# One step table, fp8 transposes and a searched end list in a fused conv-scan, linear-attention and FFN kernel

## The chip, the cores and the metric

The kernel runs on one core of a Trainium2 chip, in one launch. The metric is the device time of one execution in microseconds. The time before is 1214.04 us, the median of three runs (1212.67 to 1214.79). The engines are called PE (TensorE, with PEld for its weight loads), DVE (VectorE), ACT (ScalarE), POOL (GpSimd) and SP (SyncE, which issues most DMAs).

## The reference, cut to what matters

The input is x of 4 images, 64 x 64 positions, 96 channels, in fp32. L below is the 4096 positions of an image.

```python
# layer 0: a selective scan over the positions of an image
xn   = layernorm(group_norm(x), eps=1e-3) * gamma + beta        # (4, 4096, 96)
proj = xn @ W_in + b_in                                         # 3*96 + 3*96*16 columns
value, gate, delta = proj[:96], sigmoid(proj[96:192]), proj[192:288]
A, B, C = the rest, each (L, 96, 16)
h[t] = delta[t] * A[t] * h[t-1] + delta[t] * B[t] * value[t]    # 16 states per channel
y[t] = gate[t] * sum_over_states(C[t] * h[t])
x = x + y @ W_out + b_out
# layer 1: attention without softmax, so it is a product of small matrices
t = x as tokens
t = t + attention(layernorm(t))        # 6 heads, q @ k.T @ v, then @ Wff + bff
# feed-forward with fp8 (e5m2) operands and fp16 results
q = layernorm(t) rounded to e5m2
h = relu(fp16(fp16(q @ W1q.T) + b1q))
t = t + fp16(fp16(e5m2(h) @ W2q.T) + b2q)
```

## The kernel before

An image is cut into 8 chunks of 512 positions, so there are 32 chunks. The 96 x 16 scan states of a chunk are 12 tiles of 128 states by 512 positions (3 groups of channels times 4 groups of states). Tile number k = 12 g + r stands for tile r of chunk g, and each tile is a step of the main loop; K = 384 is the number of steps.

What one step s issues is written out by hand in the loop at the end of the kernel. On PE it is the B projection of tile s+3, the A projection of s+1 and the C projection of s, each three matmuls of 512 columns (a high and a low part; `project`, L244). On DVE it is the scan of tile s (L767), a_mul of tile s+1 (L760, it reads and writes A's PSUM bank) and c_mul of tile s (L791). On POOL it is b_mul of tile s+2 (L751). On ACT it is b_copy of tile s+3 (L748) and the copy of a scan's last state (L777). In the steps whose r is in `ON_POOL` the product with C is not made on DVE: ACT copies C's projection out (L797, c_copy) and POOL multiplies (L800, c_mul_pool). There are two PSUM banks for A, one for B, one each for even and odd C, and three (M) shared by all the other pieces. There are five buffers for b_mul's tiles (bu) and three for scans (h).

All the other work of a chunk is made of pieces which `at(step, fn)` hangs onto a step; `call(s)` issues them behind the step's own work, in the order in which they were hung. There are four kinds:

- `front`, for layer 0's input: load_x, centre and scale (group norm, POOL), stats (DVE), rstd (POOL), apply (ACT), transpose (PE), affine and upper (ACT), low (DVE and DMAs), the projections of delta, value and gate (PE, with d_out, du_out, gate_out), and the write and read through DRAM that spreads delta and delta times value over the partitions (rep). Steps count from the constant `FRONT` = -22 ahead of the chunk.
- `group_norm`: for the next image, sums over a chunk (load_gx, four transposes, two ACT passes at L509) from `SUMS` = -28.
- `gather` and `tail`: DMAs on POOL's queue that add up the four tiles of states, then state_sum and project_out (PE), gated and residual (DVE), the second layer norm (stats, rstd, apply into xa), its transpose, copy and spill to DRAM, and the gram matrix, from which `attn_matrix` makes one 97 x 96 matrix per image.
- `ffn`, an image later, since it needs that matrix: fetch, attention (L982), residual, stats, rstd, apply (L371 on ACT, L378 `apply_vector` on DVE), four fp32 transposes (L996), quant_in to fp8 (L1000), three times hidden and relu, project_out, round_out, bias_out (L1049) and total (L1055) on POOL, store. Steps count from `FFN0` = 28 behind the step at which the next image's same chunk begins.

What falls on steps from K on is not hung onto a step: it goes to the list scheduler `Plan`, object `end`. It knows each job's engine, a cost in us written in the code, what it waits for and which buffers it takes. It goes through the jobs once: it starts the one that can start first, and within `LOOK` of that time it takes the lowest rank, then the longest chain behind. The whole feed-forward of image 3 is made there. Another `Plan` makes the first six steps of the kernel.

An x tile has 15 buffers (`XBUFS`); `total` is its last reader.

Of the kernel before, what the change touches and what calls it, by code (L numbers as in the profile page):

```python
# [37 lines left out]
FRONT = -22  # L38
SUMS = -28
FFN0 = 28  # L40
ON_POOL = (1, 3, 6, 10)
# [4 lines left out]
def conv_attn_hybrid_kernel(  # L46
# [35 lines left out]
        "xn2": 1, "xq": 1, "h16": 1, "hr": 1, "hq": 1, "y16": 1, "yb": 1, "o": 1,  # L82
# [106 lines left out]
    xa_t, xal_t = [], []  # L189
    for r in range(2):  # L190
        t = const.tile([P, J, CA], F32, tag=f"xa{r}", name=f"xa{r}")
        nc.gpsimd.memset(t[:, :, C:CA], 1.0)
        xa_t.append(t)
        t = const.tile([CA, J, P], F32, tag=f"xal{r}", name=f"xal{r}")
        nc.gpsimd.memset(t[C:CA], 1.0)
        xal_t.append(t)

# [12 lines left out]
    w2_sb = sb("xn2", [C, HID], F32, "w2_sb")  # L210
# [125 lines left out]
    class LayerNorm:  # L336
# [32 lines left out]
        def apply(self, dst, src):  # L369
            for j in range(J):  # L370
                nc.scalar.activation(  # L371
                    dst[:, j, 0:C], src[:, j, :], AF.Identity,
                    bias=self.nmr[:, j : j + 1], scale=self.r[:, j : j + 1],
                )

        def apply_vector(self, dst, src):
            for j in range(J):
                nc.vector.tensor_scalar(  # L378
                    dst[:, j, 0:C], src[:, j, :], self.mv[:, j, 0:1], self.r[:, j : j + 1],
                    ALU.subtract, ALU.mult,  # L380
                )
# [5 lines left out]
    class Plan:  # L387
        HOP = 0.15
        LOOK = 0.3

# [19 lines left out]
        def run(self, fill=None):  # L410
# [13 lines left out]
            taken, back = self.taken, {}  # L424
            todo = list(self.jobs)
            while todo:
                best = None
                for n, j in enumerate(todo):
                    if any(a["end"] is None for a in j["after"]):
                        continue  # L430
                    t = self.time.get(j["engine"], 0.0)
                    for a in j["after"]:
                        hop = 0.0 if a["engine"] == j["engine"] else self.HOP
                        t = max(t, a["end"] + a["late"] + hop)
                    full = False
                    for b in j["take"]:
                        r = b.split(":")[0]
                        if len(taken[r]) >= self.rings[r]:
                            k = taken[r][-self.rings[r]]
                            full = full or k not in back  # L440
                            t = max(t, back.get(k, 0.0) + self.HOP)
                    if full:
                        continue
                    key = (t, j["rank"], -tail(j), n)
                    if best is None or t < best[0][0] - self.LOOK or (
                        t < best[0][0] + self.LOOK and key[1:] < best[0][1:]
                    ):
                        best = key, j
                (t, _, _, n), j = best
                todo.pop(n)  # L450
# [5 lines left out]
                j["end"] = self.time[e] = t + j["cost"]  # L456
                for b in j["take"]:
                    taken[b.split(":")[0]].append(b)
                for b in j["free"]:
                    back[b] = j["end"] + j["late"]  # L460
# [103 lines left out]
    def group_norm(b, s0):  # L564
# [11 lines left out]
        when = [s0 + SUMS + NT * n for n in range(NCH)]  # L576
# [119 lines left out]
    def front(b, i, s0, f=None):  # L696
        s = s0 + FRONT
        if f is None:
            f = Front(b, i)
            if (b, i) not in xt:  # L700
                at(s - 3, load_x, b, i)
            at(s, f.centre, nc.gpsimd)
            at(s + 1, f.scale, nc.gpsimd)
            at(s + 2, f.stats)
            at(s + 3, f.ln.rstd)
            at(s + 5, f.apply)
            at(s + 7, f.transpose)
            at(s + 8, f.affine)
            at(s + 9, f.upper)
            at(s + 9, f.low)  # L710
            at(s + 12, f.proj, 2)
            at(s + 13, f.d_out)
            at(s + 13, f.proj, 0)
            at(s + 14, f.du_out)
            at(s + 14, f.write)
            at(s + 15, f.read)
        at(s + 20, f.proj, 1)
        at(s + 21, f.gate_out)
# [89 lines left out]
    def state_sum(g, last=None, first=None):  # L808
# [17 lines left out]
        {"A": 2, "B": 1, "C": 1, "M": 3, "xal": 2, "xat": 1, "bu": 5, "h": 3, "rep": 2,  # L826
# [3 lines left out]
    end.last = {}  # L830

    def tail(b, i, s0):


        nm, g = f"{b}_{i}", b * NCH + i
        v, ln = {}, LayerNorm(1e-5, f"a_{nm}")
# [46 lines left out]
        def gram_add():  # L883
            nc.gpsimd.tensor_tensor(grams[b], grams[b], v["add"], ALU.add)

        plan = [
            (5, state_sum, g), (6, gated), (7, project_out), (8, residual), (8, ln.stats, t),
            (9, ln.rstd), (12, ln.apply, xa, t), (14, transpose), (15, keep), (16, spill),
            (21, gram), (22, gram_out),
        ]  # L890
        if i:
            plan.append((23, gram_add))
        for n, fn, *args in plan:
            if s0 + n < K:
                at(s0 + n, fn, *args)
        if s0 + plan[-1][0] < K:
            return
# [3 lines left out]
        job, a = end.job, None  # L901
        if s0 == K:
            for sh, late in ((0, 0.0), (2, 0.0), (3, 2.4)):
                w = job(f"wait{sh}", late, lambda: None)
                a = job("PE", 0.5, state_sum, g, sh, sh > 0, after=[a, w],
                        take=["B:y"] if sh == 0 else [])
            a = job("DVE", 0.7, gated, after=[a], free=["B:y"])
            a = job("PE", 0.5, project_out, after=[a], take=["B:o"])
            a = job("DVE", 0.56, residual, after=[a], free=["B:o"])
            a = job("DVE", 1.1, ln.stats, t, after=[a], take=[f"mv:a{i}"])  # L910
            a = job("POOL", 1.3, ln.rstd, False, after=[a])
        else:
            job("wait", 0.0, lambda: None, take=[f"mv:a{i}"])
        if s0 == K:
            applied = job("DVE", 1.3, ln.apply_vector, xa, t, after=[a], free=[f"mv:a{i}"])
        else:
            applied = job("ACT", 1.55, ln.apply, xa, t, free=[f"mv:a{i}"])
        a = job("PE", 0.4, gram, after=[applied, end.last.get("gram")], take=[f"B:g{i}"])
        end.last["gram"] = job("DVE", 0.25, gram_sum, after=[a], free=[f"B:g{i}"])
        a = job("PE", 0.45, transpose, after=[applied], take=[f"C:a{i}"])  # L920
        a = job("ACT", 0.57, keep, after=[a], free=[f"C:a{i}"], take=[f"xat:{i}"])
        end.last[b, i] = job("SP", 0.5, spill, after=[a], late=2.5, free=[f"xat:{i}"])
# [4 lines left out]
    def attn_matrix(b, s0):  # L927
# [31 lines left out]
        for n, (args, out) in enumerate(chain):  # L959
            if s0 < K:  # L960
                at(s0 + 24 + n, mm, *args)
                at(s0 + 24 + n, out)
            else:
                a = end.job("PE", 0.3, mm, *args, after=[a], take=[f"B:r{n}"])
                a = end.last["r"] = end.job("DVE", 0.25, out, after=[a], free=[f"B:r{n}"])

    def ffn(b, i, s0):
# [6 lines left out]

        def fetch():
            v["xa"] = xal_t[i % 2]
# [12 lines left out]
        def apply():  # L989
            v["xn"] = tile_of("xn2", "bu", [P, J, C], F32, "xn2")  # L990
            (ln.apply_vector if b == B - 1 else ln.apply)(v["xn"], t)

        def transpose():
            ps = v["ps"] = bank("C" if phase["end"] else "M", [C, TC], f"xq_ps_{nm}")
            for j in range(J):
                nc.tensor.transpose(ps[:, j * P : (j + 1) * P], v["xn"][:, j, :], ident)  # L996

        def quant_in():
            v["xq"] = tile_of("xq", "h", [C, TC], F8, "xq")
            nc.scalar.activation(v["xq"], v["ps"], AF.Copy, saturate=False)  # L1000
# [7 lines left out]
        def relu(m):  # L1008
            if m == 0:
# [37 lines left out]
        def bias_out():  # L1047
            v["yb"] = tile_of("yb", "xl", [P, J, C], F16, "yb")
            nc.gpsimd.tensor_tensor(  # L1049
# [3 lines left out]
        def total():  # L1053
            v["o"] = tile_of("o", "z", [P, J, C], F32, "o")
            nc.gpsimd.tensor_tensor(v["o"], t, v["yb"], ALU.add)  # L1055

        def store():
            nc.sync.dma_start(out_v[b, i], v["o"])

        plan = [  # L1060
            (min(-4, K - 4 - s0) if b < B - 1 else 0, fetch),
            (0, attention), (1, residual), (1, ln.stats, t), (2, ln.rstd),
            (5, apply), (7, transpose), (8, quant_in),
            (9, hidden, 0), (10, relu, 0), (11, hidden, 1), (12, relu, 1),
            (13, hidden, 2), (14, relu, 2), (15, project_out), (16, round_out),
            (17, bias_out), (18, total), (19, store),
        ]
        done = [fn for n, fn, *args in plan if s0 + n < K]
        for n, fn, *args in plan:
            if s0 + n < K:  # L1070
                at(s0 + n, fn, *args)
# [4 lines left out]
        end.rank = 1 + b * NCH + i  # L1076
        assert relu not in done
        if fetch in done and attention not in done:
            end.hold(f"xal:{nm}")

        def job(engine, cost, fn, *args, **kw):
            if fn not in done:
                return end.job(engine, cost, fn, *args, **kw)
            return None
# [5 lines left out]
        a = job("DVE", 1.1, ln.stats, t, after=[a], take=[f"mv:{nm}"])  # L1090
        vector = b == B - 1
        a = job("POOL", 1.3 if vector else 1.8, ln.rstd, not vector, after=[a])
        a = job("DVE" if vector else "ACT", 1.3 if vector else 1.55, apply, after=[a], take=[f"bu:x{nm}"], free=[f"mv:{nm}"])
        a = job("PE", 0.45, transpose, after=[a], take=[f"C:{nm}"], free=[f"bu:x{nm}"])
# [267 lines left out]
```

## Time and profile before

| | |
|---|---|
| median of three runs | 1214.04 us |
| profiled execution | 1214.51 us, of which the span is 1212.8 us |
| busy share of the span | PE 95%, DVE 93%, POOL 85%, PEld 72%, ACT 67% |
| mean granted TensorE clock | 0.989 |
| first scan starts, last scan ends | 30.77 us, 1135.71 us |
| chain that ended last | DVE 3%, PE 1%, POOL 1%, issue 1%; it begins at 1129.95 us |

The page gives busy time by engine, and groups of equal instructions with their count, busy time and mean length; times in groups are us, means ns. In the timeline each line has its start and its length in us, engine, line, operation and tiles. Instructions of one engine overlap: a matmul of 512 columns is shown 0.39 us long while the next starts 0.23 us behind it, so what an instruction takes of an engine is the distance to the next start. The waits name the waiting engine, line and tile, whom it waited for, the time in total, how often, and the longest.

### The profile page before, as it was taken

To read this page: it belongs to the slowest core of one execution; us is meant where nothing else is said; L and a number is where in the kernel's file an instruction comes from. 1 tells how busy PE (TensorE), PEld (TensorE's weight loads), DVE (VectorE), ACT (ScalarE), POOL (GpSimd) and SP (SyncE) were. 2 spreads that over 40 slices of the span, in tenths; PEclk is the share of its full clock that TensorE was granted. 3 is DMA by queue.
4 is the path that set the end of the run, shared out by engine and by line. 5 is a ranking of instruction groups with operands and counts; after the bars stand their busy time and mean duration, and the time that the engine had idled before them with its cause. 6 is when DMAs were issued, how large, how long until landed. Compare 5 with 4: busy or idle time off the path is not lost. (4 is left out here: it accounts for less than half of the span.)

```text
span 1212.8 us, 19189 instructions
## 1 busy us (share of the span) xinstructions
PE 1155.5 (95%) x5888; PEld 872.8 (72%) x5888; DVE 1125.7 (93%) x2103; ACT 809.9 (67%) x1812; POOL 1031.6 (85%) x1171
## 2 busy tenths in 40 slices
PE   6899999999999999999999999999999999999884
PEld 5677777777777777777777777677777777777652
DVE  6799999999999999999999999999999999999794
ACT  4655656655565787777777777777777777776574
POOL 3988878888888888999999888999999899988654
PEclk8999999999999999999999999999999999999998
DMA  7656767677776676677667766766776667666221
GB/s 185 141 133 145 165 151 164 147 161 164 168 160 151 153 166 151 154 168 176 159 151 164 172 154 146 174 154 149 154 174 154 154 158 174 153 145 142 66 66 40
DMA packets 104289, 182.14 MB, mean 150 GB/s; under 512 B 42637, under 2 KB 50769, under 8 KB 104186
## 3 DMA queue, kind: packets, MB, share of 16 engines
q1 hardware_dynamic: 90060, 106.96, 36.5%
q0 software_dynamic: 13536, 73.93, 30.2%
q8 instruction: 47, 0.77, 0.3%
q14 instruction: 56, 0.46, 0.1%
q10 hardware_dynamic: 590, 0.02, 0.0%
HBM read 69.12 MB, written 24.77 MB: 77 GB/s over the span
## 5 line engine op out<-in xcount | busy, mean ns | idle before, releaser
L751 POOL TENSOR_TENSOR bu<-bu,rep 128x512 f32<-128x512 f32 x384 | 557.7, 1496 | 14.7 <-ACT bu L748 9.2
L748 ACT ACTIVATE bu<-Bps,b_bac 128x512 f32<-128x512 f32 x384 | 263.7, 687 | 286.0 <-PE Bps L244 269.0
L767 DVE TENSOR_TENSOR_SCAN h<-Aps,state,bu 128x512 f32<-128x512 f32 x336 | 426.4, 1269 | 13.2 <-POOL bu L751 3.5
L760 DVE SCALAR_TENSOR_TENSOR Aps<-Aps,b_bac,rep 128x512 f32<-128x512 f32 x384 | 282.5, 736 | 25.1 <-PE Aps L244 24.6
L244 PE MATMUL Bps<-xs,w 128*128 128x512 f32 x768 | 268.1, 430 | 3.7 <-ACT bu L748 3.4
L244 PE MATMUL Aps<-xs,w 128*128 128x512 f32 x768 | 249.6, 406 | 14.2 <-DVE h L767 13.3
L800 POOL TENSOR_TENSOR ch<-ch,h 128x512 f32<-128x512 f32 x128 | 193.5, 1512 | 2.6 <-ACT ch L797 2.4
L244 PEld LDWEIGHTS Aps<-xs,w 128*128 128x128 f32 x768 | 138.6, 189 | 70.5 <-DVE h L767 42.3
L244 PEld LDWEIGHTS Bps<-xs,w 128*128 128x128 f32 x768 | 129.4, 191 | 46.5 <-issue 24.3
L244 PE MATMUL Aps<-xl,w 128*128 128x512 f32 x384 | 152.6, 397 | 0.3 <-DMA w<-w 0.3
L244 PE MATMUL Bps<-xl,w 128*128 128x512 f32 x384 | 151.8, 395 | 0.0
L244 PE MATMUL Dps<-xs,w 128*128 128x512 f32 x384 | 121.1, 397 | 0.0
L244 PE MATMUL Cps<-xs,w 128*128 128x512 f32 x384 | 120.8, 395 | 0.0
L806 POOL DMA_DIRECT2D ch<-ch x94 | 89.0, 947 | 15.1 <-DMA ch<-ch 11.5
L791 DVE SCALAR_TENSOR_TENSOR ch<-Dps,b_bac,h 128x512 f32<-128x512 f32 x128 | 94.7, 740 | 0.5 <-PE Dps L244 0.4
L791 DVE SCALAR_TENSOR_TENSOR ch<-Cps,b_bac,h 128x512 f32<-128x512 f32 x128 | 95.0, 742 | 0.0
L244 PEld LDWEIGHTS Aps<-xl,w 128*128 128x128 f32 x384 | 72.4, 188 | 18.4 <-DMA w<-w 1.0
L244 PEld LDWEIGHTS Bps<-xl,w 128*128 128x128 f32 x384 | 72.5, 189 | 17.5
L244 PEld LDWEIGHTS Dps<-xs,w 128*128 128x128 f32 x384 | 72.4, 189 | 17.5
L244 PEld LDWEIGHTS Cps<-xs,w 128*128 128x128 f32 x384 | 72.3, 188 | 17.5
L244 PE MATMUL Dps<-xl,w 128*128 128x512 f32 x192 | 76.0, 396 | 0.0
L244 PE MATMUL Cps<-xl,w 128*128 128x512 f32 x192 | 75.7, 394 | 0.0
(196 smaller groups left out, 2056.0 us busy)
## 6 DMA issues: line engine op xcount, KB each, us to landing
ch<-ch POOLq DMA_DIRECT2D x94, 768.0 KB, 6.5
rep<-ddd SPq DMA_DIRECT2D x124, 384.0 KB, 6.4
ddd<-dd SPq DMA_DIRECT2D x31, 384.0 KB, 3.0
xl<-lo SPq DMA_DIRECT2D x62, 128.0 KB, 2.4
x<-in_x_dram SPq DMA_DIRECT2D x32, 192.0 KB, 2.9
xatd<-xat SPq DMA_DIRECT2D x32, 192.0 KB, 3.1
xal<-xatd SPq DMA_DIRECT2D x32, 192.0 KB, 5.8
out_dram<-o SPq DMA_DIRECT2D x32, 192.0 KB, 2.1
```

The costliest lines, as they stand in the source:

```text
L244: nc.tensor.matmul(ps, lhsT=wt[:, n], rhs=mv, start=(n == 0), stop=(n == 2))
L748: nc.scalar.activation(self.bu, self.b_ps, AF.Identity, bias=self.bias(0))
L751: nc.gpsimd.tensor_tensor(self.bu, self.bu, rep[self.b, self.i][:, 1, self.cg], ALU.mult)
L760: nc.vector.scalar_tensor_tensor(self.a_ps, self.a_ps, self.bias(1), rep[self.b, self.i][:, 0, self.cg], ALU.add, ALU.mult,)
L767: nc.vector.tensor_tensor_scan(self.h, self.a_ps, self.bu, 0.0 if self.i == 0 else state[self.sh, self.cg], ALU.mult, ALU.add,)
L791: nc.vector.scalar_tensor_tensor(self.slot(), self.c_ps, self.bias(2), self.h, ALU.add, ALU.mult)
L800: nc.gpsimd.tensor_tensor(self.ch, self.ch, self.h, ALU.mult)
L806: nc.gpsimd.dma_start(chs[g, 0], chs.pop((g, sh)), accum_op=ALU.add)
```

## The change

1. `FRONT`, `SUMS`, `FFN0` and the steps written in the functions are replaced by one table `AT`, with a step for each piece; nearly every piece gets another step. `ON_POOL` is (0, 2, 7, 8) instead of (1, 3, 6, 10).
2. In the feed-forward, apply writes fp8 directly (two lasting tiles xn8 of 128 x 4 x 128, zeroed once), and the four transposes are fp8 matmuls with an fp8 identity; quant_in reads the first 96 partitions. hidden 1 runs at step 31, a while ahead of hidden 0 and 2.
3. `Plan.run` makes its list by a function `schedule(bias, look)`; for the end it tries 800 lists with random ranks added and keeps the one whose last job ends first by the costs. The costs of several jobs differ, all ffn chunks of four share a rank, and the rules for what falls into the end are by groups (`place`).
4. In the end, the feed-forward's norm of image 3 is applied by DVE for even chunks and by ACT for odd ones, where DVE had all; bias_out and total of the last two chunks are on DVE.
5. The start's `LOOK` is 0.6 instead of 0.8.

```diff
-FRONT = -22
-SUMS = -28
-FFN0 = 28
-ON_POOL = (1, 3, 6, 10)
+AT = {
+    "load_x": -39, "centre": -25, "scale": -24, "stats": -22, "rstd": -22, "apply": -21,
+    "transpose": -14, "affine": -13, "upper": -13, "low": -12, "proj_d": -9, "d_out": -9,
+    "proj_u": -9, "du_out": -9, "write": -9, "read": -6, "proj_gate": -3, "gate_out": -1,
+    "gather1": 7, "gather2": 11, "gather3": 14,
+    "state_sum": 18, "gated": 18, "project_out": 19, "residual": 19, "stats_a": 20,
+    "rstd_a": 21, "apply_a": 22, "transpose_a": 33, "keep": 34, "spill": 39, "gram": 24,
+    "gram_out": 24, "gram_add": 26,
+    "fetch": 21, "attention": 26, "residual_f": 26, "stats_f": 26, "rstd_f": 27, "apply_f": 29,
+    "transpose_f": 30, "quant_in": 31, "hidden0": 37, "relu0": 37, "hidden1": 31, "relu1": 33,
+    "hidden2": 38, "relu2": 38, "project_f": 40, "round_out": 40, "bias_out": 40, "total": 46,
+    "store": 51,
+    "sums": -31,
+}
+ON_POOL = (0, 2, 7, 8)
...
+        vector = b == B - 1 and i % 2 == 0
...
         def apply():
-            v["xn"] = tile_of("xn2", "bu", [P, J, C], F32, "xn2")
-            (ln.apply_vector if b == B - 1 else ln.apply)(v["xn"], t)
+            v["xn"] = next_of(xn8_t, "xn8")
+            (ln.apply_vector if vector else ln.apply)(v["xn"], t, saturate=False)

         def transpose():
-            ps = v["ps"] = bank("C" if phase["end"] else "M", [C, TC], f"xq_ps_{nm}")
+            ps = v["ps"] = bank("C" if phase["end"] else "M", [P, TC], f"xq_ps_{nm}")
             for j in range(J):
-                nc.tensor.transpose(ps[:, j * P : (j + 1) * P], v["xn"][:, j, :], ident)
+                nc.tensor.matmul(
+                    ps[:, j * P : (j + 1) * P], lhsT=v["xn"][:, j, :], rhs=ident8,
+                    start=True, stop=True,
+                )
...
+            last_two = phase["end"] and b == B - 1 and i > NCH - 3
...
+            rng = random.Random(1)
+            best = zero = [0.0] * len(self.jobs)
+            lates = schedule(zero, self.LOOK)
+            for n in range(self.tries):
+                wide = n < self.tries // 4
+                share, size = (1.0, rng.choice((0.5, 2.0, 5.0))) if wide else (0.02, 2.0)
+                bias = [
+                    b + rng.gauss(0.0, size) if rng.random() < share else b
+                    for b in (zero if wide else best)
+                ]
+                found = schedule(bias, rng.choice((0.05, 0.15, self.LOOK)))
+                if found and (lates is None or found[0] < lates[0]):
+                    lates, best = found, bias
...
-        a = job("DVE" if vector else "ACT", 1.3 if vector else 1.55, apply, after=[a], take=[f"bu:x{nm}"], free=[f"mv:{nm}"])
+        a = job("DVE" if vector else "ACT", 1.9 if vector else 1.8, apply, after=[a], take=[f"xn8:{nm}"], free=[f"mv:{nm}"])
...
-            r.append(job("DVE", 0.3, relu_vector, m, after=[c]))
+                r.append(job("DVE", 0.5, relu_vector, m, after=[c]))
...
-        plan.LOOK = 0.8
+        plan.LOOK = 0.6
```

In the table, steps of `front` and `sums` count from the chunk's own first step; those of `tail` too, and those of `ffn` from the first step of the same chunk of the next image.

## The prediction

> **What bounds the kernel now.** I read the page's first part, then the stages as windows, then the timeline of VectorE and of TensorE inside one chunk, then the waits, and last the groups and the timeline of the end.
>
> ```profile
> PE 1155.5 (95%) x5888; PEld 872.8 (72%) x5888; DVE 1125.7 (93%) x2103; ACT 809.9 (67%) x1812; POOL 1031.6 (85%) x1171
> ```
> ```profile
> 0.00:72.54 72.54, 59.01 (x260) 45.48 (x261) 52.84 (x99) 40.74 (x81) 47.33 (x65) 0.91 0.68 158
> 72.54:306.75 234.21, 228.70 (x1079) 172.36 (x1078) 225.90 (x377) 135.23 (x326) 200.76 (x216) 1.00 0.70 155
> 306.75:584.03 277.28, 271.43 (x1371) 206.44 (x1370) 264.92 (x480) 189.93 (x440) 246.47 (x279) 1.00 0.71 159
> 584.03:864.50 280.47, 276.19 (x1430) 210.76 (x1429) 268.20 (x498) 207.52 (x469) 256.92 (x295) 1.00 0.72 160
> 864.50:1135.71 271.21, 267.71 (x1378) 201.75 (x1376) 262.31 (x472) 192.51 (x432) 244.62 (x274) 1.00 0.68 152
> 1135.71:1212.80 77.09, 52.48 (x381) 35.97 (x378) 51.54 (x183) 44.00 (x69) 35.49 (x48) 0.91 0.20 54
> ```
> The windows are cut at first scans of images: start with chunk 0, seven chunks of image 0, eight each of images 1, 2, 3, and what follows the last scan (after the length: busy PE, PEld, DVE, ACT, POOL, then clock, DMA). A chunk takes 234.21/7 = 33.5 us, then 34.7, 35.1 and 33.9. The granted clock is 1.00 there. Two engines sit at 95% and above, so I cost both by the distance from one start to the next.
>
> ```profile
> 699.95 0.63 PE L244 MATMUL Cps<-xs,w 128*128 128x512 f32 x2
> 700.42 0.40 PE L244 MATMUL Cps<-xl,w 128*128 128x512 f32 x1
> 700.65 1.03 PE L982 MATMUL a_ps<-rmat,xal 97*128 97x96 f32 x8
> 701.46 0.71 PE L244 MATMUL Bps<-xs,w 128*128 128x512 f32 x2
> 702.01 0.40 PE L244 MATMUL Bps<-xl,w 128*128 128x512 f32 x1
> ```
> ```profile
> 719.66 0.73 DVE L760 SCALAR_TENSOR_TENSOR Aps<-Aps,b_bac,rep 128x512 f32<-128x512 f32 x1
> 720.52 1.28 DVE L767 TENSOR_TENSOR_SCAN h<-Aps,state,bu 128x512 f32<-128x512 f32 x1
> 721.72 0.74 DVE L760 SCALAR_TENSOR_TENSOR Aps<-Aps,b_bac,rep 128x512 f32<-128x512 f32 x1
> 722.36 0.75 DVE L791 SCALAR_TENSOR_TENSOR ch<-Dps,b_bac,h 128x512 f32<-128x512 f32 x1
> 723.02 0.68 DVE L631 TENSOR_TENSOR lo<-xnt_ps,xs 96x512 fp32r<-96x512 f32 x1
> 723.62 1.27 DVE L767 TENSOR_TENSOR_SCAN h<-Aps,state,bu 128x512 f32<-128x512 f32 x1
> ```
> On PE a projection of three matmuls takes 0.70; a piece takes its own pitch (a_ps 0.81) and 0.08 more, as the two matmuls behind it need 0.55 where Cps needs 0.47. On DVE a scan takes 1.20, a_mul 0.64, c_mul 0.66, lo 0.60. Where a scan follows a_mul at once, that pair takes 0.86: a bubble of 0.22. It is there in steps whose c_mul is on POOL and which have no DVE piece.
>
> ```profile
> PEld Aps L244 <- DVE h L767: 42.3, 73, 3.1
> DVE Aps L760 <- PE Aps L244: 24.6, 39, 1.4
> ```
> These two waits are mutual: PE waits for a scan to free one of two A banks, and DVE waits for that bank's matmuls.
>
> Sums for a chunk of images 1 and 2, other pitches from the same timeline. DVE: 12 x 1.84 + 8 x 0.66 + lo 0.60, dd 0.66, yg 0.60, two residuals 0.58, three statistics 0.94 = 33.2, and three bubbles 0.66 = 33.8. PE: 36 projections 25.2, three narrow ones 2.1, four groups of transposes (xnt, xat, xq, gx) 0.44 each, a_ps 0.90, o_ps 0.90, gram 0.70, y_ps 1.08, three h 0.69, second layer 0.58 = 33.9. POOL's sum is 31.3 and ACT's 27.7. So PE and DVE are both the bound, and 0.8 to 1.2 of each chunk is one waiting for the other.
>
> **The table of steps.** It moves every piece, so it changes loads by step, not sums. DVE by step 0 to 11, before: 2.5, 2.1, 2.5, 2.1, 4.1, 4.0, 2.4, 2.5, 4.0, 2.5, 2.1, 3.1; PE: 2.1, 2.3, 3.2, 3.0, 3.0, 3.4, 2.1, 3.6, 2.5, 3.2, 2.8, 2.5. DVE's heavy steps (4, 5, 8; 12.1 in sum) stand against 8.9 on PE, and the light ones behind them against PE's heavy 7 and 9; with two A banks PE can't run ahead to even that out. After, DVE: 2.4, 2.5, 4.3, 3.2, 2.5, 2.5, 3.1, 2.4, 2.8, 2.5, 2.5, 2.5; PE: 2.8, 2.3, 3.2, 3.5, 2.7, 2.5, 3.5, 3.2, 2.1, 3.2, 2.5, 2.1. The four POOL steps (0, 2, 7, 8) are those with lo, statistics, residual and statistics, so something stands between a_mul and scan everywhere: three bubbles gone, 0.66 of DVE. Only step 2 is uneven, and step 3 repays it.
>
> POOL's own queue: steps 2 and 3 hold two b_mul, one c_mul, gather3, rstd_c, gram_add and rstd_f: at pitches of 1.25, 0.69, 1.9 for a root with its shift and 0.35, that is 8.6 against DVE's 7.5; b_mul is issued two steps ahead of its scan, which covers that 1.1. SP's queue: load_x moves from step -25 to -39, while the total that frees its buffer is issued at the equivalent of -38, so SP waits one to two steps, and fetch and load_gx queue behind it. Fetch has five steps, 13.8 us, to attention, and lands in 5.8: covered, by about 2.5; without cover attention waits by the excess. The read of rep (landing 6.4) at -6 is needed at -2: 11 us, covered.
>
> A new wait: apply_f at 29 and transpose_f at 30 are one step apart where there were two. In images 1 and 2 ACT does the gx sums (1.39) and then four pieces of apply (pitch 0.36, 1.44) in step 5; with 0.25 of hops xn8 is ready 3.1 after gx, and PE is there after three projections, 2.2. PE waits some 0.75 at xq (its four transposes follow ACT piece by piece), and y_ps and the next B projection queue behind it; a_mul waits two steps on. Bounds: 0 (PE late) and 0.95.
>
> **The fp8 transposes.** Four fp32 ones have a pitch of 108 ns; the fp8 row nearest (L1035, 96 columns) has 43 ns, so 57 for 128: 0.31 with the 0.08 instead of 0.44. I take 0.13 off PE, bounds 0 and 0.16: PE 33.75. Writing fp8 from ACT is not dearer (hq 631 ns against hr 722 for 512). Cover for ident8 and two memsets at the start: POOL is busy 10 of the first 30 us; uncovered 1 us (memset rows 519 ns).
>
> **The chunks, summed.** Image 0 has neither a_ps, h, second layer nor xq: PE 31.3, DVE 32.3 before, 31.7 after, measured 33.5, excess 1.2. Its excess after lies between 0 and 1.1; I take 0.5, as the columns match better: 32.2, 7 x 1.3 = 9. Images 1 and 2: measured 34.9; after 33.75 with no wait, 35.6 with the new wait and the whole old excess; I take 33.75 + 0.65 = 34.4: 16 x 0.45 = 7. Image 3 has no gx, so no such wait: PE 33.3, DVE 33.2, I take 33.5 against 33.9: 8 x 0.4 = 3. Together 19; bounds: 35 gained (no excess anywhere: 13, 18, 5), and 13 lost (images 1 and 2 at 35.6 with nothing elsewhere, 16 x 0.7 = 11, and 2 at the start, whose list also changes while POOL is its fullest engine, 47.3 of 72.5 us, with c_mul on it in other steps).
>
> **The end.**
> ```profile
> L378 DVE TENSOR_SCALAR xn<-x,mv_f,rstd_f 128x96 f32<-128x96 f32 x32 | 14.0, 501 | 0.0
> ```
> ```profile
> 1183.38 2.93 DVE L378 TENSOR_SCALAR xn<-x,mv_f,rstd_f 128x96 f32<-128x96 f32 x4
> 1190.62 1.70 DVE L378 TENSOR_SCALAR xn<-x,mv_f,rstd_f 128x96 f32<-128x96 f32 x4
> ```
> ```profile
> ACT hq L1029 <- DVE h L1025: 13.8, 10, 2.6
> ```
> DVE is busy 51.5 of 77.1, ACT 44.0. A piece of the norm takes 324 ns in the median but up to 1060, and those long ones lie beside POOL's work (at 1183.38 POOL does yb and o throughout). Half of the 32 pieces go to ACT: DVE loses 16 x 0.50 = 8.0 and gains four additions of 0.55 (bias and total of the last two chunks) = 2.2, so 45.7 (fp8 written from VectorE has no such row; a piece lies between the median 0.32 and the long 1.06, I keep 0.50); ACT gains 16 x 0.36 = 5.8, so 49.8. The largest load falls from 51.5 to 49.8, the list is packed with durations nearer to these rows (norm 1.3 becomes 1.9, relu 0.3 becomes 0.5; rows: 2.0 and 0.51), and ACT's 13.8 of waiting for relus is what a better order can take. The head (gram to rmat) and the tail (last hq to the end, 9.8) stay. I take 5 off, bounds 10 off and 6 on (ACT bound: its whole added load shows).
> [...]
> [...]
>
> **The rivals.** (1) Forecast: 19 + 5 = 24 off the profiled execution's 1214.5 (span 1212.8 and 1.7 around it; 0.5 above the median of 1214.0, within its runs): 1190. (2) PE decides alone: images 1 and 2 keep 34.8, since PE's sum falls by 0.13 only; then bubbles and image 0 give 5, the end 1: 1208. For it: PE's 99% in those windows; against: 1.0 per chunk is idle by the sums. (3) Slower: the xq wait. If rstd_f reaches ACT so late (behind step 2's gather and step 3's b_mul and c_mul on POOL) that the wait is 2.3 in 24 chunks, 55 is lost against a gain of 37 without any wait (9 + 16 x 1.15 + 8 x 0.6 + 5): 1233. It decides from 37/24 = 1.5 per chunk. Against: POOL is done with rstd_f about 2.5 before ACT gets to it. (4) The searched list doesn't carry over: the end 6 longer, and the chunks give as much: 1214.
>
> Chances: (1) 0.70, (2) 0.16, (3) 0.10, (4) 0.04. The first two are faster by over 0.2% (2.4 us, about what a measurement of this kernel can tell): 0.86; within it 0.04; slower 0.10. The range reaches from 1172 (most of both bounds of gain) to 1212, past the second case, leaving out (3) and (4) and the best of (1).
>
> **What would show it.** Right: image windows at 7 x 32.2, 8 x 34.4, 8 x 33.5; no scan 0.86 behind its a_mul; the two mutual waits well below half; PE waiting for ACT xn at xq, 0.7 a time, in images 1 and 2 alone; 16 vector norm pieces in the end and about 72 us behind the last scan. Wrong: chunks of image 3 at 33.9 or more, a wait of POOL's that ends a scan's, or an xq wait over 1.5.

## The result and the profile after

The changed kernel takes 1201.68 us, the median of four runs (1200.2 to 1203.03), against 1213.96 for the kernel before: a ratio of 0.990, 95% interval 0.9882 to 0.9917. The forecast was 1190.0, in a range of 1172 to 1212. The profiled execution took 1200.81 us, its span 1199.1. So half of the forecast gain came. The busy times of the engines, from the profile's first part:

```profile
PE 1148.7 (96%) x5899; PEld 876.9 (73%) x5899; DVE 1110.0 (93%) x2091; ACT 817.8 (68%) x1828; POOL 1032.2 (86%) x1178
```

The stages of the changed kernel as windows, cut at the same scans as before: start, image 0 (seven chunks), images 1, 2 and 3 (eight each), end.

```profile
0.00:77.16 77.16, 59.48 (x259) 46.08 (x260) 52.59 (x98) 40.02 (x79) 50.35 (x70) 0.87 0.65 147
77.16:308.70 231.54, 225.33 (x1076) 172.27 (x1076) 225.07 (x378) 136.66 (x328) 199.68 (x215) 1.00 0.73 157
308.70:583.63 274.93, 271.61 (x1375) 207.90 (x1374) 262.39 (x481) 193.98 (x446) 247.09 (x279) 1.00 0.72 160
583.63:860.38 276.75, 274.30 (x1427) 210.42 (x1426) 265.35 (x499) 208.02 (x468) 256.39 (x294) 1.00 0.73 162
860.38:1126.40 266.02, 263.16 (x1373) 201.49 (x1374) 260.06 (x473) 190.39 (x425) 244.32 (x272) 1.00 0.70 155
1126.40:1199.10 72.70, 54.85 (x399) 38.70 (x393) 44.55 (x171) 48.72 (x86) 34.42 (x52) 0.86 0.22 61
```

The lengths, before and after, set beside the terms of the sum:

| stage | before | after | measured | forecast |
|---|---|---|---|---|
| start | 72.54 | 77.16 | +4.6 | 0 |
| image 0 | 234.21 | 231.54 | -2.7 | -9 |
| images 1 and 2 | 557.75 | 551.68 | -6.1 | -7 |
| image 3 | 271.21 | 266.02 | -5.2 | -3 |
| end | 77.09 | 72.70 | -4.4 | -5 |
| span | 1212.8 | 1199.1 | -13.7 | -24 |

Two terms carry the whole shortfall: the start, and image 0. The other three are within 2.2 us each.

What the table of steps was to do is in the trace. The two mutual waits (whole span; time, times, longest) fell from 42.3 and 24.6:

```profile
PEld Aps L269 <- DVE h L824: 3.7, 8, 1.5
DVE Aps L817 <- PE Aps L269: 12.6, 16, 3.6
```

And in a step whose c_mul is on POOL, another piece now stands between a_mul (L817) and the scan (L824). VectorE's timeline in chunk 7:

```profile
278.18 0.73 DVE L817 SCALAR_TENSOR_TENSOR Aps<-Aps,b_bac,rep 128x512 f32<-128x512 f32 x1
278.82 0.68 DVE L694 TENSOR_TENSOR lo<-xnt_ps,xs 96x512 fp32r<-96x512 f32 x1
279.42 1.27 DVE L824 TENSOR_TENSOR_SCAN h<-Aps,state,bu 128x512 f32<-128x512 f32 x1
```

a_mul keeps its 0.64, lo its 0.60. Of the 384 scans 5 still start 0.85 to 0.94 behind their a_mul, four of them in chunk 0 and one in chunk 31; before, 82 started 0.83 to 0.89 behind it, nearly all in steps 2, 4 and 11. Chunks 6 and 7 of image 0, which have nothing special in them, last 31.7 us each (distance between first scans) where they lasted 32.8: less than the 32.2 of the forecast, and the bare DVE sum. Before, such a chunk had the three bubbles (0.66) and one wait of a_mul for A's matmuls (0.47 and 0.54 in these two chunks); after, it has neither, and that is about the 1.1. But chunks 1 to 5 last 32.8, 34.1, 32.5, 33.9 and 34.8, together 9.6 over five clean ones; before, the same five stood 4.6 over. So 7 x 1.1 = 7.7 was gained in image 0 and 5.0 given back.

### The profile page after: what moved, and what is told of

It reads as the page before. It is cut to its first block, busy times and chain, and to the rows that moved or that the text cites. A ratio compares the mean times of both kernels' runs of the same rounds, so it can differ in the third digit from the quotient of the medians.

```text
span 1199.1 us, 19211 instructions
## 1 busy us (share of the span) xinstructions
PE 1148.7 (96%) x5899; PEld 876.9 (73%) x5899; DVE 1110.0 (93%) x2091; ACT 817.8 (68%) x1828; POOL 1032.2 (86%) x1178
## 5 line engine op out<-in xcount | busy, mean ns | idle before, releaser
L808 POOL TENSOR_TENSOR bu<-bu,rep 128x512 f32<-128x512 f32 x384 | 512.3, 1342 | 53.6 <-ACT state L834 38.5
L824 DVE TENSOR_TENSOR_SCAN h<-Aps,state,bu 128x512 f32<-128x512 f32 x336 | 426.0, 1268 | 0.6 <-POOL ch L857 0.5
L817 DVE SCALAR_TENSOR_TENSOR Aps<-Aps,b_bac,rep 128x512 f32<-128x512 f32 x384 | 281.8, 734 | 12.6 <-PE Aps L269 12.6
L269 PE MATMUL Aps<-xs,w 128*128 128x512 f32 x768 | 242.4, 396 | 1.2 <-DVE h L824 1.1
L857 POOL TENSOR_TENSOR ch<-ch,h 128x512 f32<-128x512 f32 x128 | 172.5, 1348 | 14.1 <-ACT ch L854 10.7
L269 PEld LDWEIGHTS Aps<-xs,w 128*128 128x128 f32 x768 | 143.6, 188 | 38.0 <-DVE h L824 3.7
L269 PEld LDWEIGHTS Bps<-xs,w 128*128 128x128 f32 x768 | 126.5, 191 | 61.1 <-ACT bu L805 26.3
L848 DVE SCALAR_TENSOR_TENSOR ch<-Dps,b_bac,h 128x512 f32<-128x512 f32 x160 | 118.6, 741 | 0.8 <-PE Dps L269 0.7
L854 ACT ACTIVATE ch<-Cps,b_bac 128x512 f32<-128x512 f32 x96 | 65.8, 685 | 22.9 <-PE Cps L269 22.9
```

The costliest lines, as they stand in the source:

```text
L269: nc.tensor.matmul(ps, lhsT=wt[:, n], rhs=mv, start=(n == 0), stop=(n == 2))
L808: nc.gpsimd.tensor_tensor(self.bu, self.bu, rep[self.b, self.i][:, 1, self.cg], ALU.mult)
L817: nc.vector.scalar_tensor_tensor(self.a_ps, self.a_ps, self.bias(1), rep[self.b, self.i][:, 0, self.cg], ALU.add, ALU.mult,)
L824: nc.vector.tensor_tensor_scan(self.h, self.a_ps, self.bu, 0.0 if self.i == 0 else state[self.sh, self.cg], ALU.mult, ALU.add,)
L848: nc.vector.scalar_tensor_tensor(self.slot(), self.c_ps, self.bias(2), self.h, ALU.add, ALU.mult)
L854: nc.scalar.activation(self.ch, self.c_ps, AF.Identity, bias=self.bias(2))
```

## The experiments

The runs are told by question. Differences of stages are between profiled executions; ratios are to the kernel before.

**1. The start.** In the changed kernel ACT's timeline has one long wait at the start (the bracket: idle before, and who ended it); the second line is the same instruction before.

```profile
59.46 1.54 ACT L396 ACTIVATE z<-z,nmr_c,rstd_c 128x96 f32<-128x96 f32 x4 [8.13 <-POOL nmr_c L384]
```
```profile
57.33 1.55 ACT L371 ACTIVATE z<-z,nmr_c,rstd_c 128x96 f32<-128x96 f32 x4 [0.65 <-POOL nmr_c L359]
```

It is the first norm's apply of chunk 2. The table has it at -21, so at step 24 - 21 = 3. The main loop begins at step 6, and whatever hangs on earlier steps is issued in one burst ahead of it; before, the piece was at step 7. ACT stands 8.1 us for POOL's norm, with b_copy and so the next B projection queued behind it (TensorE's longest wait for bu there is 7.4).

```diff
-            at(s0 + AT[name], fn, *args)
+            late = 4 if (b, i, name) == (0, 2, "apply") else 0
+            at(s0 + AT[name] + late, fn, *args)
```

> The changed kernel with one piece of one chunk moved: the first norm's apply of chunk 2 is issued at step 7, where it stood before the change, in place of step 3. Theory: at step 3 it is issued in the burst ahead of the main loop, ACT stands 8.1 us waiting for POOL's shift of that norm, and the copies of B's projections behind it make TensorE (7.4) and VectorE (3.6) wait; moved back, the start up to chunk 1's first scan falls from 77.2 to about 72.8 us, the whole by 4, about 1197.5. Rival: the start is set by POOL (50 of its 77 us busy, products with C in other steps than before), so the ACT wait only changes its place: 77 stays, about 1201.5.

Measured 1197.95 us, ratio 0.9866 (0.9849 to 0.9883); the start 72.6, every other stage within 1.0 of the changed kernel's. The cause is shown: one ACT piece put ahead of its data made the start of this pair 4.6 us longer. A part of the 4.6 is TensorE's clock, whose granted mean in the start is 0.87 without the edit and 0.93 with it (0.91 in the kernel before). Eight other runs without the edit had starts of 75.1 to 77.0, three more with it 72.4 to 73.6, two of these at a granted 0.88, so its worth is about 3 to 4.

**2. The wait at xq.** TensorE's wait for the fp8 norm, in the window of images 1 and 2 of the changed kernel:

```profile
PEld L1085 <- ACT xn L396: 12.0, 43, 0.3
```

12.0 over 16 chunks is 0.75 a chunk. This is time of the weight loads. What TensorE itself loses is read from the distance between starts, from the last matmul of Cps to y_ps: it is 0.56 without a wait (every chunk of image 3) and 1.52 in most of chunks 10 to 20, 0.94 more in the mean of these eleven. Chunks 8 and 9 have no xq transposes yet, and 21 to 23 have no sums and no wait. Over the two images that is 10.3 us. The prediction's reason was that the gx sums stand ahead of apply on ACT, in the same step. To take them out of it:

```diff
-    "sums": -31,
+    "sums": -28,
```

> The changed kernel with the group-norm sums of images 2 and 3 three steps later (-28 in place of -31, so step 8 of a chunk in place of 5). Theory: in images 1 and 2 the xq transposes wait because ACT makes the sums (1.39 us) ahead of the norm's four pieces; with the sums gone from step 5 that wait goes, and the 16 chunks fall from 34.5 to about 33.8 each: images 1 and 2 together from 551.7 to 541 us, the whole 10 us shorter than the changed kernel, about 1191. Image 0, image 3, the start and the end stay within 1 us. Rival (TensorE's sum alone sets the chunk): the wait turns up at another place, the two images stay within 2 us, about 1201. Second rival (step 8 is no better a place): longer, over 1203.

Measured 1194.26 us, ratio 0.9833 (0.9818 to 0.9848). Of the waits for the same transposes, over the whole span, the line is now

```profile
  ACT xn L396: 2.1, 7
```

and images 1 and 2 last 545.3 instead of 551.7. The same group of transposes in chunk 19, in the changed kernel and in this run:

```profile
706.84 0.40 PE L269 MATMUL Cps<-xl,w 128*128 128x512 f32 x1
707.13 1.30 PE L1085 MATMUL xq_ps<-ident,xn 128*128 128x128 fp8e5 x4
```
```profile
700.55 0.40 PE L269 MATMUL Cps<-xl,w 128*128 128x512 f32 x1
700.79 0.40 PE L1085 MATMUL xq_ps<-ident,xn 128*128 128x128 fp8e5 x4
```

The distance is at most 0.57 in every chunk now. So the wait is gone, but of TensorE's 10.3 only 6.3 came off the time. The window of image 2:

```profile
579.11:852.85 273.74, 273.17 (x1428) 209.41 (x1427) 266.39 (x498) 207.55 (x469) 257.57 (x296) 1.00 0.74 165
```

PE is now busy for 273.17 of 273.74 us, and a chunk takes about 34.2. That TensorE's own work is what sets it now is likely but not shown by this share: matmuls overlap (Cps above is 0.40 long, and the next can start 0.24 behind it), and in the changed kernel the same window had 274.30 of 276.75 busy, an idle of 2.45, while the xq groups alone held TensorE up by 4.6. Where the other 4.0 went was not followed further.

**3. The fp8 transposes.** The four fp32 transposes were put back into the changed kernel, with apply writing fp32 and quant_in reading as before.

```diff
-                nc.tensor.matmul(
-                    ps[:, j * P : (j + 1) * P], lhsT=v["xn"][:, j, :], rhs=ident8,
-                    start=True, stop=True,
-                )
+                nc.tensor.transpose(ps[:, j * P : (j + 1) * P], v["xn"][:, j, :], ident)
```

> The changed kernel with the four transposes of the feed-forward in fp32 again, as before the change (the norm writes fp32 into the two lasting tiles, the transposes take the fp32 identity, quant_in rounds to fp8). Theory: 0.13 us of TensorE per chunk in images 1 to 3 where TensorE is the bound, 3 us in all, about 1204.5, with nothing in image 0. Rival (the fp8 form is a larger part, through a shorter wait at xq or cheaper writes): 8 us or more. Rival (hidden): within 1 us of 1201.5.

Measured 1206.32 us, ratio 0.9941 (0.9924 to 0.9958), 4.6 slower than the changed kernel. Images 1 to 3 are 0.5, 1.0 and 1.6 longer, 3.1 in all, which is the sum of the prediction's 0.13 in 24 chunks. But no chunk shows 0.13. The distance from Cps to y_ps is 0.76 with fp32 and 0.56 with fp8 where nothing waits, so 0.20 in the eight chunks of image 3 and in three of image 2. In the eleven chunks that wait for ACT it is 1.61 and 1.52 in most, so 0.09: there the transposes follow ACT's pieces, 0.36 apart, and a shorter one saves little. The rest of the 4.6 is in image 0 (1.6), where no such transposes run, so it does not belong to them: chunk 5 varies from run to run (below).

**4. The choice of POOL steps.** The changed kernel with the old choice:

```diff
-ON_POOL = (0, 2, 7, 8)
+ON_POOL = (1, 3, 6, 10)
```

> The changed kernel with the old choice of steps whose product with C is made on GpSimd (1, 3, 6, 10 for 0, 2, 7, 8). The sums of all engines stay as they are. Theory (what image 0's clean chunks and image 3 gained comes from the match of VectorE's and TensorE's loads by step, and from having something between a_mul and scan in every step): the bubbles of 0.22 come back in two to four steps and step 2 carries 4.96 on VectorE, so a clean chunk of image 0 is 32.4 to 33.2 instead of 31.7 and image 3's 33.9 to 34.8 instead of 33.5; the whole 15 to 35 us slower than the changed kernel. Rival (TensorE alone decides, the choice is indifferent): clean chunks within 0.2 of 31.7 and 33.5, the whole within 5 us.

Measured 1238.29 us, ratio 1.019 (1.0166 to 1.0214): 37 us slower, a little over the theory's upper end. Clean chunks of image 0 take 33.4, those of image 3 34.3. VectorE's timeline has the bubble back (a_mul, and the scan 0.86 behind it):

```profile
352.42 0.73 DVE L817 SCALAR_TENSOR_TENSOR Aps<-Aps,b_bac,rep 128x512 f32<-128x512 f32 x1
353.29 1.22 DVE L824 TENSOR_TENSOR_SCAN h<-Aps,bu 128x512 f32<-128x512 f32 x1
```

No engine has other work to do in this run. Which steps put the product on POOL belongs to the table as much as the steps of the pieces do. The run changes the bubbles and the match of the loads together, so it does not part the two; and TensorE's granted clock was 0.50 for 13.6 us of its images 0 and 1, which is a part of the 37.

**5. Image 0: first guesses.** Image 1's group-norm sums have steps of their own there.

```diff
-            when = [8, 15, 22, 29, 36, 43, 50, 57]
+            when = [13, 17, 25, 29, 37, 41, 49, 53]
```

> The changed kernel with the group-norm sums of image 1 at steps 13, 17, 25, 29, 37, 41, 49, 53 (steps 1 and 5 of chunks 1 to 4) in place of 8, 15, 22, 29, 36, 43, 50, 57. Theory: these steps were written by hand for the old table and not moved with it; in chunks 1 to 5 they fall on full steps, so those chunks take 32.5 to 34.8 us where chunks 6 and 7 take 31.7. With the sums in light steps the seven chunks of image 0 fall from 231.5 to about 226 us (a part of the excess is the late weights' at step 8 and the end of the start), the whole to about 1196. Rival (a backlog from the start decides in chunks 1 to 5): within 1 us of 231.5, about 1201.5.

Measured 1199.09 us, ratio 0.988 (0.9865 to 0.9894), image 0 unchanged at 231.46. A miss as a whole, and telling in its parts: chunk 2 went from 34.1 to 32.5, chunk 4 from 33.9 to 36.1, with a step 8 of 6.39 us in it. So the sums at step 22 did cost 1.6, and something in step 8 was worth more. Next, the chain that ends the group norm:

```diff
-        for n, name in ((1, "moments"), (2, "mean"), (4, "root"), (6, "diagonal"), (8, "spread"),
-                        (8, "spread_out")):
+        for n, name in ((1, "moments"), (2, "moments_pool"), (3, "mean"), (4, "mean_pool"), (5, "root"),
+                        (6, "root_pool"), (7, "diagonal"), (8, "spread"), (9, "spread_out")):
```

> The changed kernel, but of the next image's group-norm chain (moments, mean, root) the GpSimd operations are issued one step behind the VectorE operations that they read, so that GpSimd's queue does not stand waiting for VectorE with the layer norms of the running chunks behind it; the chain then ends one step later. Theory (the waiting of GpSimd's queue is what costs chunks 4 and 5 of image 0 their extra 5.3 us over the clean 31.7): these two chunks 65.0 to 66.5 us instead of 68.7, and chunk 13 34.9 to 35.5 instead of 36.8; the whole 3 to 6 us faster than the changed kernel. Rival (the chain's own matmuls and VectorE operations, and the late weights of step 56, are the cost): chunks 4 and 5 stay at 68 to 69.5 in sum, the whole within 1.5 us.

Measured 1197.61 us, ratio 0.9859 (0.9836 to 0.9882). Chunks 4 and 5 sum to 68.1, as the rival says. The whole is 4.1 under the changed kernel, in the theory's range, but not by these two chunks: every stage but image 3 is 0.5 to 0.9 shorter, with chunk 13 at 35.7 for 36.8 (the theory had 34.9 to 35.5) and chunk 21 at 33.8 for 34.9. Chunk 5 fell from 34.8 to 33.0, but chunk 4 rose from 33.9 to 35.1, since a VectorE scaling of 96x2 numbers took 1.43 us in it where it takes 0.17 elsewhere. Then the late conversions of weights:

```diff
-        at(NT + 8 + NT * n, fn)
+        at((47, 71, 83, 95)[n], fn)
```

> The changed kernel, but the four late conversions of weights, which fall on steps 20, 32, 44 and 56 (step 8 of chunks 1 to 4; there step 8 lasts 2.92, 3.39, 3.20 and 4.84 us against the clean 2.76, 3.3 more in all), fall on steps 47, 71, 83 and 95 (step 11 of chunks 3, 5, 6 and 7), where VectorE and TensorE are light. Theory (they cost that much because step 8 is now a full step of VectorE): steps 8 are 2.76 again and steps 11 grow by less than half as much; image 0 228.5 to 230.0 us instead of 231.5. Rival (their own work shows wherever it lies, or the wait behind them only moves): image 0 231 to 232.5.

Measured 1201.90 us, ratio 0.9905 (0.9888 to 0.9923), image 0 235.22: both theories missed. Steps 8 are 2.76 again, but the steps 11 grew by 0.2, 0.5, 0.4 and, with the biases' conversions at step 95, by 3.7. A step with VectorE time to spare did not take them for nothing. Image 0 also has a chunk 5 of 36.7 for 34.8 in this run, for a reason told under 6.

**6. Together, and what the long steps are.**

```diff
-    "sums": -31,
+    "sums": -28,
...
+            late = 4 if (b, i, name) == (0, 2, "apply") else 0
+            at(s0 + AT[name] + late, fn, *args)
```

> The sums at -28 and chunk 2's first-norm apply four steps later, together. Theory (the two causes lie in different stages, so they add): start 72.6, image 0 231.5, images 1 and 2 271.6 and 273.8, image 3 266.1, end 71 to 72.5; median 1186 to 1188.5. Rival (the later apply or the shifted sums only move a wait that the other then pays): over 1191.

Measured 1190.03 us, ratio 0.9793 (0.9767 to 0.9819): 11.7 under the changed kernel, where the two edits alone gave 7.4 and 3.7. They add, as the theory says; the median is above its range since image 0 took 233.2, with a chunk 5 of 35.9. That chunk is 34.8 in some runs and 36.3 in others of kernels whose instructions there are the same. The trace shows what the 1.5 us are. In steps 4 and 5 of that chunk TensorE stands idle for 2.3 to 2.8 us, until ACT copies a B projection out. Behind it the run without the search (section 7) and the changed kernel go on like this (after the length: busy PE, PEld, DVE, ACT, POOL, then granted clock, DMA):

```profile
226.10:229.50 3.40, 3.40 (x12) 2.78 (x12) 2.11 (x3) 0.86 (x3) 1.77 (x2) 0.50 0.76 166
```
```profile
226.10:229.50 3.40, 3.40 (x19) 2.87 (x18) 2.62 (x3) 2.15 (x6) 2.06 (x2) 1.00 0.61 149
```

At a granted clock of 0.50 the distance between two matmuls of 512 columns is 0.43 where it is 0.23 at 1.00, and the stretch lasts 3.4 us: an estimate of 1.7 us lost. Every run with a chunk 5 of 35.9 or more has such a stretch there (this run too); the changed kernel, the run with the later apply and the run with the shifted sums have none behind idles of 2.74, 2.75 and 2.37. The run without the search had an idle of 2.74 too; what decides it is not shown.

Then together with the split chain, the moved weights, and image 1's sums in a mixture of the two lists:

```diff
+    "sums": -28,
...
+            when = [13, 17, 25, 29, 36, 43, 50, 57]
...
+        for n, name in ((1, "moments"), (2, "moments_pool"), (3, "mean"), (4, "mean_pool"), (5, "root"),
+                        (6, "root_pool"), (7, "diagonal"), (8, "spread"), (9, "spread_out")):
...
+            late = 4 if (b, i, name) == (0, 2, "apply") else 0
...
+        at((47, 71, 83, 95)[n], fn)
```

> Everything that helped, together: sums at -28, chunk 2's first-norm apply four steps later, GpSimd's part of the group-norm chain a step behind VectorE's, the late weights at steps 47, 71, 83 and 95, and image 1's first three sums at steps 13, 17 and 25 instead of 8, 15 and 22. Theory (each is a cost in its own place): start 72.6 to 73.6, image 0 226 to 229, images 1 and 2 about 271 and 273.2, image 3 266.1, end 70.6 to 72; median 1181 to 1186. Rival (in image 0 the pieces only trade places): image 0 230.5 to 233, median 1187 to 1190.

Measured 1189.06 us, ratio 0.9792 (0.9777 to 0.9806); image 0 231.35. The rival by the numbers, but not by its reason: chunks 1 to 5 sum to 162.5 instead of 168.1, and step 95 alone lasts 7.62. Its VectorE line and what POOL did meanwhile:

```profile
298.80 4.63 DVE L356 CAST b_q<-b 128x3 f32<-128x3 fp8e5 x1
```
```profile
298.71 1.28 POOL L684 TENSOR_TENSOR z<-x,gmr 128x384 f32<-128x384 f32 x1
299.69 1.54 POOL L826 TENSOR_TENSOR bu<-bu,rep 128x512 f32<-128x512 f32 x1
300.93 1.25 POOL L687 TENSOR_TENSOR z<-z,gmr 128x384 f32<-128x384 f32 x1
301.90 1.49 POOL L826 TENSOR_TENSOR bu<-bu,rep 128x512 f32<-128x512 f32 x1
```

A cast of three numbers per partition takes 4.63 us, from 298.80 to 303.43. POOL runs four products without a gap, and the last ends at 303.39. The same two casts of the biases in the changed kernel, at step 56, and the two POOL products beside them:

```profile
199.85 0.64 DVE L356 CAST b_q<-b 128x3 f32<-128x3 fp8e5 x1
...
200.63 1.18 DVE L359 CAST b_q<-b 128x96 f32<-128x96 fp8e5 x1
```
```profile
199.19 1.28 POOL L808 TENSOR_TENSOR bu<-bu,rep 128x512 f32<-128x512 f32 x1 [0.64 <-ACT state L834]
200.43 1.32 POOL L857 TENSOR_TENSOR ch<-ch,h 128x512 f32<-128x512 f32 x1
```

POOL's ends are at 200.47 and 201.75, VectorE's at 200.49 and 201.81. In the kernel before the second cast found POOL idle and took 0.21. The run with image 1's sums moved had the first at 3.17, ended 0.03 behind POOL's third product; the scaling of 1.43 ended 0.03 behind a POOL product too. So these casts and this scaling, which read and write SBUF alone, each ended 0.02 to 0.06 behind a POOL product that ran beside them. It is not every VectorE operation on SBUF: the 384 statistics of the layer norms (BATCH_NORM_STATS2) in the changed kernel, SBUF to SBUF too, took 0.23 to 0.26 each, with POOL 86% busy. The last run puts the three such conversions on ACT, in the same step, and leaves the group-norm chain of images 2 and 3 as it was:

```diff
-        nc.vector.tensor_copy(b1_q, b1_8)
+        nc.scalar.copy(b1_q, b1_8)
...
-        nc.vector.tensor_copy(b2_8, b2_sb, saturate=False)
-        nc.vector.tensor_copy(b2_q, b2_8)
+        nc.scalar.activation(b2_8, b2_sb, AF.Copy, saturate=False)
+        nc.scalar.copy(b2_q, b2_8)
```

> The run of everything together with two edits: three of the late conversions of fp8 biases, which read and write SBUF alone, are on ScalarE instead of VectorE (a cast of 128x3 elements took 4.63 us there at step 95, ended 0.04 us behind the last of GpSimd's back-to-back products, and step 95 was 7.62 us long), and the GpSimd part of the group-norm chain is a step late for image 1 only (for images 2 and 3 it had made chunks 13 and 21 1.3 and 1.5 us longer). Theory (a VectorE operation from SBUF to SBUF waits until GpSimd's running products are done): step 95 is 2.5 to 3.3 us long, image 0 226.2 to 228 us, images 1 and 2 271.6 and 273.8, median 1182 to 1185.5. Rival (the bias conversions wait for their transposes or their data, or the place is bad whatever runs there): step 95 over 5 us, image 0 over 229.5, median over 1186.

Measured 1186.39 us, ratio 0.9764 (0.975 to 0.9777): the fastest version. The cast, on ACT:

```profile
299.43 0.19 ACT L356 CAST b_q<-b 128x3 f32<-128x3 fp8e5 x1 [1.09 <-DVE b L355]
```

It takes 0.19, beside a POOL as busy as before; step 95 is 2.60, image 0 226.39. The theory held there and in image 2 (273.8). The median is 0.9 over its range, and over the 1186 of the rival: image 1 came to 272.6, 1.0 over, and the end to 72.9, where the two runs before had 70.6 and 71.2. Image 1's 1.0 is most likely the price of the three casts on ACT: they stand ahead of the copies of the next chunk's input, VectorE waits 0.81 for one of these, and the first two steps of chunk 8 last 3.28 and 3.07, where the first run of this section has 2.37 and 2.72.

**7. The end.** First the search alone, then the sharing of the norm alone, undone.

```diff
-    end.tries = 800
+    end.tries = 0
```

> The changed kernel with the end's list made in one pass with the new costs, without the 800 tries. Theory (the search is what took the end from 77.1 to 72.7): the end 75 to 78 us, the whole 2 to 5 us slower than the changed kernel. Rival (the norm shared by two engines and the corrected costs did it): the end 72 to 74, the whole within 1.5 us.

Measured 1202.17 us, ratio 0.989 (0.9867 to 0.9914), the end 73.0: the rival.

```diff
-        vector = b == B - 1 and i % 2 == 0
+        vector = b == B - 1
```

> The changed kernel with the norm of image 3's feed-forward in the end on VectorE for all chunks, as before the change; the search and the costs stay. Theory (the sharing of the norm is what shortened the end, as the run without the search left it at 73.0): VectorE's load in the end rises from 44.6 to about 52 us again and the end is 75 to 77.5 us instead of 72.7. Rival (the new costs, or the two additions on VectorE, or what reaches the end earlier, did it): the end 72 to 74.

Measured 1200.44 us, ratio 0.9886 (0.987 to 0.9903), the end 71.3: the rival again. The norm's group in the end, changed kernel and this run:

```profile
L403 DVE TENSOR_SCALAR xn<-x,mv_f,rstd_f 128x96 fp8e5<-128x96 f32 x16 | 6.0, 439 | 0.0
```
```profile
L403 DVE TENSOR_SCALAR xn<-x,mv_f,rstd_f 128x96 fp8e5<-128x96 f32 x32 | 11.3, 414 | 1.7 <-POOL rstd_f L392 1.7
```

Sharing took 5.3 us of norm off VectorE and the end was no shorter for it. The changed kernel and eight of the other runs, with one and the same list, had ends of 70.6 to 72.9, so a worth of about 1 us can't be told. VectorE is busy 49.1 of 71.3 in that run and is not what bounds the end. ACT's wait for VectorE's relus is short there too:

```profile
ACT hq L1121 <- DVE h L1117: 4.6, 4, 2.1
```

It was 13.8 before. So neither the search nor the sharing is needed for the 4.4 by itself; what is left are the new costs, the groups that fall into the end, the additions on VectorE, or that either of the two does without the other, as no run left out both. Which of these it is stays open.

## Why the prediction was right and wrong

**The table, in clean steps: right, and a little better than forecast.** The mutual waits fell from 66.9 to 16.3, of 82 bubbles 5 are left, and image 0's clean chunk is 31.7: its excess after, taken as 0.5, was 0 there. Image 3 came to 33.25 a chunk for 33.5. The clean chunks show both causes, three bubbles and a wait at the A bank, 0.66 and 0.5; the run with the old POOL steps shows that the gain hangs on these steps. The median of 1201.7 alone would not tell the first case (1190) from the second (1208); these stages do, since the second has 34.8 a chunk for images 1 and 2 and no gain from image 3, which gave 5.2. (The prediction's bounds of gain, 13, 18 and 5, make 36 and not 35; nothing hangs on it.)

**Images 1 and 2: the cause right, the size in part by luck.** 34.4 was forecast, 34.4 and 34.6 measured. The new wait at xq is there, with the gx sums as its cause, but it holds TensorE up 0.94 (worked out: 0.75, at most 0.95), and only in 11 of the 16 chunks: 0.64 over all, beside the 0.65 of the sum. And of the 10.3 us only 6.3 came off when the wait went, so it did not cost the time as much as TensorE lost at it; that the rest is TensorE's own sum, the second case's mechanism, is likely but not shown. The slower case needed 1.5 in each of 24 chunks.

**fp8: the total right by luck,** 3.1 measured in images 1 to 3 for 24 x 0.13. The 0.13 set 0.31, which has the 0.08 behind a piece in it, against 0.44, which has not. Without the 0.08 on either side it is four times 108 less 57 ns, 0.20, and that is what the chunks without a wait show; the eleven with one show 0.09.

**Image 0: the mis-sized term, 9 for 2.7.** The step that failed is the term "7 x 1.3 = 9". It took a mean over seven chunks for seven equal ones. Five of them hold one-time work: late weights, image 1's sums and its group-norm chain. Its surplus grew from 4.6 to 9.6. By steps, 3.3 of it lies in step 8 of chunks 1 to 4 (the weights), 1.7 at the head of chunk 2 (the sums), 3.0 in steps 4 to 7 of chunk 5 (the chain). The prediction has no price for these pieces, but the new table changed the steps where they hang and what POOL does beside them. The bias casts alone went from 0.51 to 1.82. A full step is not the whole reason, since in lighter steps the weights cost 4.8 in place of 3.3 as long as the bias casts ran on VectorE. The rows show how such a cast fares beside POOL: on VectorE one took 4.63, as long as four POOL products in a row ran, and on ACT 0.19 beside a POOL as busy. What makes the one wait and the other not is not shown by any run.

**The start: 0 for +4.6.** The list of the start was named as a risk of 2, with POOL's c_mul as the reason. The reason was wrong: a single ACT piece fell on a step ahead of the main loop, which was worth 3 to 4 of the 4.6. A look at every piece of the first three chunks with a step under `START` would have found it: 24 - 21 is 3.

**The end: the size right (72.7 for 72), the reason not.** VectorE's load fell to 44.6 (forecast 45.7) and ACT's rose to 48.7 (49.8), but "the largest load falls" was no bound: undoing the sharing changed nothing that can be told. The norm's long pieces, seen beside POOL's work in the prediction, look like the casts' wait: in the end of the kernel before all nine pieces over 0.9 end 0.07 us behind a POOL instruction, and the others take 0.30 to 0.35. The four additions on VectorE, costed at 0.55, take 0.55, 0.56, 1.03 and 1.15, 0.82 in the mean; the two long ones ran beside a POOL instruction and ended 0.42 behind it.

## What to carry to other kernels

When a table moves pieces, cost the clean chunk and the special chunks apart: a mean over a stage hides one-time work, and its price depends on the step that it falls on. Check each piece whose step lies ahead of the loop's first step, since ACT, waiting 8.1 us there, held up the B projections behind it. Put small VectorE casts and scalings from SBUF to SBUF where GpSimd is idle, or on ScalarE (one of 128x3 took 4.63 us beside GpSimd's products, 0.19 on ScalarE), and look at what then stands behind them there. Before a cost per piece is taken from two rows, see that both count the same things.

## What the runs showed of the hardware that was not expected

A VectorE cast of 128x3 numbers took 0.17 us (GpSimd idle, the run with the old POOL steps) to 4.63 us by what GpSimd was doing, and the same cast took 0.19 on ScalarE. It does not always get in between two GpSimd products: at 0.64 it ended with the first of two, at 4.63 with the last of four. A chunk with the same instructions took 34.8 or 36.3 us in different runs: behind the same idle of 2.74 us TensorE's granted clock was 1.00 in one and 0.50 for 3.4 us in the other. Between the first scan of chunk 1 and the last scan of image 3, the idles of TensorE ahead of such stretches were 1.9 to 3.7 us in all runs together, and idles of 2.37 to 2.75 are among those that had none behind them.
